# Three-layer graph convolution and neighbour dilation on one core: every engine held in program order, chained steps spread over the TensorE schedule, two comparisons made one

## The chip, the cores and the metric

The kernel runs on one core of one Trainium2 chip. The metric is device time in microseconds (us). A core has five engines that run side by side and meet at semaphores: TensorE (PE; its weight loads are listed as PEld), VectorE (DVE), ScalarE (ACT), GpSimd (POOL) and SyncE (SP), which here only issues DMAs. [...]

## The reference, cut to what matters

There are 16 graphs (batches) of 1024 nodes with 128 features, and for each a symmetric 1024 x 1024 adjacency matrix `adj`, about 6% filled.

```python
h = relu(layernorm(x))
for W, b, last in layer0:                 # 3 convolutions
    h = h @ W + b
    nh = h / max(|h|, 1e-12)
    h = (adj * (nh @ nh.T)) @ h           # relu unless last
x = x + h
h = relu(layernorm(x))
# dilation, row by row: of a row with num > 10 neighbours, those whose
# running count is a multiple of ceil(num / 2) are dropped, in row and column;
# later rows see it
adj_d = dilate(adj)
h1..h3 = three sage layers on adj_d       # batch norm after each
x = x + concat(h1, h2, h3) @ Wl + bl
```

## The kernel before, in words

**Two stages.** Stage one, up to line 720, holds all of layer 0 and all of the dilation, interleaved. Stage two, from line 723, holds the three sage layers; the change does not touch its code. The dilation depends on `adj` alone, so it fills engines while layer 0 keeps TensorE at work.

**Layer 0.** `order` lists 48 convolutions (16 batches in pairs, 3 layers each). A convolution goes through eight steps `s`, one for each block row `q` of the symmetric product, in the order `SEQ`. `products` (L290) multiplies on PE into PSUM `pg`, ACT copies `pg` to `g` (L311), and POOL multiplies `g` with the adjacency into `ew` (L312). `turn` (L320) transposes `g` on PE into PSUM `gt` (two buffers), and DVE multiplies it into the other part of `ew` (L330). `sums` and `sums_back` (L337, L353) multiply `ew` into the one PSUM tile `po`, three steps after the products (`LAG = 3`). After the last step ACT empties `po` (`hTo`, L368). Around this lie the transposes of the adjacency (`adjT_tile`, L216), which POOL stores to DRAM, the layer norm, the residual, and the features of the next convolution.

**The dilation.** It goes through 16 stretches: 8 row blocks `k`, each for two halves of 8 batches. A stretch has three parts. *Patterns*, 8 times: ACT makes the 0/1 pattern (L548, L549), PE transposes what earlier blocks kept (`pk`), DVE joins both (L554). *Rounds*, 2 to 6: DVE compares 8 tables (`E`, L611), PE counts (`pc`), DVE corrects `x` (L640). *Ranking*, 8 times: DVE subtracts the removals (L667), a DVE scan makes the running count `rank` (L670), ACT centres it (L671), DVE makes `kp` with two comparisons (L674, L677), POOL stores it as `keep` (L678).

**What sets the order.** `layer0()` and `dilation()` are generators. `layer0` yields the microseconds of PE work it just wrote (`COLS = 0.215` for a block of 128 columns, `TURN = 0.109` for a transpose), the dilation yields weights, and the loop at L701 writes layer-0 steps until they have caught up. So the program text is one interleaving. Only the PE calls of stage one are marked `keep_in_program_order` (L159 to L164). On DVE, ACT, POOL and SP a scheduler with its own idea of durations chose the final order.

Of the kernel before, what the change touches and what calls it, by code (L numbers as in the profile page):

```python
# [35 lines left out]
LAG = 3  # L36
# [6 lines left out]
T_DIL = 10  # L43


@with_exitstack
def tile_adj_preln_d2(
# [61 lines left out]
    def layernorm_relu(pool, dst, src, nm):  # L109

        st = pool.tile([P, NCH, 6], F32, tag="ln_st", name=f"ln_st_{nm}")
        mv = pool.tile([P, NCH, 2], F32, tag="ln_mv", name=f"ln_mv_{nm}")
        for c in range(NCH):
            nc.vector.bn_stats(st[:, c, :], src[:, c, :])
            nc.vector.bn_aggr(mv[:, c, :], st[:, c, :])
        rstd = pool.tile([P, NCH], F32, tag="ln_rstd", name=f"ln_rstd_{nm}")
        nc.scalar.activation(rstd, mv[:, :, 1], AF.Sqrt, bias=eps_col)
        nc.vector.reciprocal(rstd, rstd)
        nmr = pool.tile([P, NCH], F32, tag="ln_nmr", name=f"ln_nmr_{nm}")
        nc.vector.scalar_tensor_tensor(nmr, mv[:, :, 0], -1.0, rstd, ALU.mult, ALU.mult)  # L120
        for c in range(NCH):
            nc.scalar.activation(
                dst[:, c, :], src[:, c, :], AF.Relu, bias=nmr[:, c : c + 1], scale=rstd[:, c : c + 1]
            )

# [16 lines left out]
    def transposed(psum_pool, dst, src, nm, func=AF.Copy, halves=range(NHALF), transpose=nc.tensor.transpose):  # L142

        for h in halves:
            pt = psum_pool.tile([P, CPH, P], F32, tag="sm", name=f"pt_{nm}_{h}")
            for c in range(CPH):
                transpose(pt[:, c, :], src[:, h * CPH + c, :], ident)  # L147
            nc.scalar.activation(dst[:, h * CPH : (h + 1) * CPH, :], pt, func)


    with ExitStack() as actx:
# [6 lines left out]

        def matmul(*args, **kwargs):  # L159

            tc.keep_in_program_order(nc.tensor.matmul(*args, **kwargs))  # L161

        def transpose(*args):
            tc.keep_in_program_order(nc.tensor.transpose(*args))  # L164
# [12 lines left out]
        for fill, value, op in ((0.0, -2.0, ALU.is_ge), (4.0 * FAR, 2.0 * FAR, ALU.is_gt)):  # L177
            up = pool2.tile([P, NCH, P], F32, tag="tt", name=f"up_{fill}")[:, 0, :]
# [15 lines left out]
        mfl = pool2.tile([P, NCH, P], F32, tag="tt", name="mfl")[:NB, 0, :]  # L194
# [11 lines left out]

        adjA = pool1.tile([P, 2, NCH, N], F32, name="adjA")
        Nat = {}

        def adj_piece(b, q):  # L210
            Nat[b, q] = nat = pool2.tile([P, NCH, P], F32, tag="nat", name=f"nat_{b}_{q}")
            nc.sync.dma_start(
                nat, adj[b][:, q * P : (q + 1) * P].rearrange("(c p) q -> p c q", p=P)
            )

        def adjT_tile(b, q):  # L216

            t = adjA[:, b % 2, q, :]
            transposed(
                ps_sm, t.rearrange("p (c q) -> p c q", q=P), Nat.pop((b, q)), f"a{b}_{q}", transpose=transpose  # L220
            )
            nc.gpsimd.dma_start(adjT_d[b][q], t)

        class Batch:
# [6 lines left out]
            def fetch(self):  # L231
                b = self.b
                self.xb = pool2.tile([P, NCH, D], F32, tag="xb", name=f"xb_{b}_{self.l}")
                nc.sync.dma_start(self.xb, x[b].rearrange("(c p) d -> p c d", p=P))

            def norm(self):
                b = self.b
                self.h = pool2.tile([P, NCH, D], F32, tag="tt", name=f"h_{b}")
                layernorm_relu(pool2, self.h, self.xb, f"l0_{b}")

            def enter(self, h):
                if h == 0:
                    self.hT = pool2.tile([P, NCH, P], F32, tag="hT", name=f"hT_{self.b}")
                transposed(ps_sm, self.hT, self.h, f"h{self.b}", halves=(h,), transpose=transpose)

            def features(self, h):
# [6 lines left out]
                for c in range(CPH):  # L253
                    matmul(
                        pw[:, c, :], lhsT=self.hT[:, h * CPH + c, :], rhs=w0[:, l, :], start=True, stop=True
                    )
                if rn is None:
                    nc.vector.tensor_tensor(
                        self.hN[:, hc, :], pw, b0[:, l : l + 1, :].to_broadcast([P, CPH, P]), ALU.add
                    )  # L260
                else:
                    for c in range(CPH):
                        n = h * CPH + c
                        nc.vector.scalar_tensor_tensor(
# [3 lines left out]
            def turned(self):  # L268

                nhT = pool1.tile([P, NCH, P], F32, tag="nhT", bufs=2, name=f"nhT_{self.b}_{self.l}")  # L270
                transposed(ps_sm, nhT, self.hN, f"n{self.b}_{self.l}", transpose=transpose)
                self.next_nhT = nhT.rearrange("p c q -> p (c q)")

            def scaled(self):

                nm = f"{self.b}_{self.l}"
                hS = pool1.tile([P, NCH, D], F32, tag="hS", bufs=2, name=f"hS_{nm}")
                ss = pool2.tile([P, NCH], F32, tag="in_ss", name=f"ss_{nm}")
                for c in range(NCH):
                    nc.scalar.activation(hS[:, c, :], self.hN[:, c, :], AF.Square, accum_out=ss[:, c : c + 1])  # L280
                self.rn = inv_root(pool1, ss, nm)
                nc.gpsimd.tensor_tensor(
                    hS, self.hN, self.rn.unsqueeze(2).to_broadcast([P, NCH, D]), ALU.mult
                )
                self.next_hS = hS

            def begin(self):
                self.nhT, self.hS = self.next_nhT, self.next_hS

            def products(self, s):  # L290
# [9 lines left out]
                g = pool1.tile([P, most, P], F32, tag=f"g{s % 2}", name=f"g_{nm}")  # L300
                for c in range(0, row, CPH):
                    n = min(CPH, row - c)
                    pg = ps_g.tile([P, CPH, P], F32, tag="pg", name=f"pg_{nm}_{c}")
                    matmul(
# [6 lines left out]
                    nc.scalar.activation(g[:, c : c + n, :], pg[:, :n, :], AF.Copy)  # L311
                nc.gpsimd.tensor_tensor(  # L312
# [5 lines left out]
                return ew, g  # L318

            def turn(self, s, ew, g):  # L320
# [3 lines left out]
                for c in range(1, row, CPH):  # L324
                    n = min(CPH, row - c)
                    pt = ps_t.tile([P, CPH, P], F32, tag="gt", name=f"gt_{self.b}_{self.l}_{q}_{c}")
                    for i in range(n):
                        transpose(pt[:, i, :], g[:, c + i, :], ident)
                    at = row + c - 1
                    nc.vector.tensor_tensor(  # L330
# [6 lines left out]
            def sums(self, s, ew):  # L337

                q = SEQ[s]
                if s == 0:  # L340
                    self.po = ps_o.tile([P, N], F32, tag="po", name=f"po_{self.b}_{self.l}")
                for h in range(q // CPH, NHALF):
                    c = max(q, h * CPH)
                    n = (h + 1) * CPH - c
                    matmul(
# [7 lines left out]
            def sums_back(self, s, ew):  # L353
# [4 lines left out]
                for n in range(1, NCH - q):  # L358
                    matmul(
# [6 lines left out]
                if s == NCH - 1:  # L366
                    self.hT = pool2.tile([P, NCH, P], F32, tag="hT", name=f"hTo_{self.b}_{self.l}")
                    nc.scalar.activation(  # L368
# [4 lines left out]
            def residual(self):  # L373
                b = self.b
                self.x2 = x2 = pool2.tile([P, NCH, D], F32, tag="tt", name=f"x2_{b}")
                for h in range(NHALF):
                    pt = ps_sm.tile([P, CPH, P], F32, tag="sm", name=f"px_{b}_{h}")
                    for c in range(CPH):
                        transpose(pt[:, c, :], self.hT[:, h * CPH + c, :], ident)
                    for c in range(CPH):  # L380
                        n = h * CPH + c
                        nc.vector.scalar_tensor_tensor(
                            x2[:, n, :], pt[:, c, :], self.rn[:, n : n + 1], self.xb[:, n, :], ALU.mult, ALU.add
                        )
                nc.gpsimd.dma_start(x2_d[b].rearrange("(c p) d -> p c d", p=P), x2)

            def next_layer(self):
                b = self.b
                h0 = pool2.tile([P, NCH, D], F32, tag="tt", name=f"h0_{b}")
                layernorm_relu(pool2, h0, self.x2, f"l1_{b}")  # L390
# [649 lines left out]
```

## Time and profile before

| what | value |
|---|---|
| median of 3 runs | 3395.79 us (3391.37 to 3405.93) |
| profiled execution | 3385.13 us; its span on the core 3383.3 us |
| PE / DVE / ACT / POOL busy over the span | 2877.8 / 2105.8 / 1442.5 / 1052.7 us |
| stage one | 0 to about 2072 us of the span |
| PE / DVE / ACT / POOL busy, 0 to 2090 us | 1737 / 1417 / 1162 / 885 us |
| mean granted TensorE clock | 0.931 of full speed |

The span runs from the first to the last instruction; the run has 2 us around it. A group of instructions is listed by line, engine and operation, with its busy time and the mean time of one; the idle time behind it is that of the engine just before such an instruction. The granted clock is the share of full speed that TensorE was given.

### The profile page before, as it was taken

Reading aid. Unit: us, or ns where it says so; the run is one execution under the profiler, and the core shown is the slowest. Engines: PE = TensorE matmul, PEld = TensorE weight load, DVE = VectorE, ACT = ScalarE, POOL = GpSimd, SP = SyncE. Lnnn points to the kernel's source line nnn. Section 1 sums busy time; section 2 is a strip of 40 time slices with the busy share of each in tenths; the row PEclk is TensorE's granted clock in tenths of the full one; section 3 lists DMA queues with packets and bytes.
Section 4 is the critical chain, followed back from the end, with each engine's and each line's share of the span. In section 5 each row is a group of like instructions: output and inputs, shape, how many; then the busy total and the mean of one; then the engine's idle time right before and its main releaser. Section 6 shows DMA issues by size and latency. Waiting matters only on the chain. (4 is left out here: it accounts for less than half of the span.)

```text
span 3383.3 us, 53792 instructions
## 1 busy us (share of the span) xinstructions
PE 2877.8 (85%) x19811; PEld 2352.0 (70%) x19811; DVE 2105.8 (62%) x5319; ACT 1442.5 (43%) x3445; POOL 1052.7 (31%) x940
## 2 busy tenths in 40 slices
PE   6887888897797888788888897778887999989996
PEld 4655666565565665566656575777876899989996
DVE  2866767856867867876896733566666233345555
ACT  6746755655555545555645532011111322222223
POOL 2453444444344344444444443111211001000000
PEclk9998998998998999899899998889998999999998
DMA  8326336336336336427616303999997566656663
GB/s 279 120 84 219 122 112 223 102 113 208 102 105 208 121 101 214 135 90 222 198 43 193 129 1 117 352 345 354 351 353 278 181 205 203 204 181 225 225 224 125
DMA packets 436788, 623.10 MB, mean 184 GB/s; under 512 B 80080, under 2 KB 309328, under 8 KB 436512
## 3 DMA queue, kind: packets, MB, share of 16 engines
q1 hardware_dynamic: 349936, 416.87, 38.5%
q0 software_dynamic: 52288, 185.43, 14.3%
q10 hardware_dynamic: 34288, 17.24, 1.8%
q8 instruction: 158, 2.59, 0.3%
q14 instruction: 118, 0.97, 0.1%
HBM read 426.51 MB, written 192.94 MB: 183 GB/s over the span
## 5 line engine op out<-in xcount | busy, mean ns | idle before, releaser
L161 PE MATMUL po<-ew,hS 128*128 128x128 f32 (+3 forms) x3840 | 832.0, 353 | 68.5 <-ACT hTo L368 63.9
L312 POOL TENSOR_TENSOR ew<-g,adjA 128x1024 f32<-128x1024 f32 (+7 forms) x384 | 612.3, 1598 | 563.9 <-issue 262.5
L161 PEld LDWEIGHTS po<-ew,hS 128*128 128x128 f32 x3840 | 550.5, 199 | 212.1 <-issue 134.2
L161 PE MATMUL pg<-nhT 128*128 128x512 f32 (+3 forms) x1152 | 474.7, 523 | 23.9 <-ACT g L311 23.6
L963 PE MATMUL agg<-hw,aT 128*128 128x128 f32 x4096 | 472.0, 275 | 0.0
L963 PEld LDWEIGHTS agg<-hw,aT 128*128 128x128 f32 x4096 | 466.7, 192 | 4.0
L330 DVE TENSOR_TENSOR ew<-gt,adjA 128x512 f32<-128x512 f32 (+1 forms) x480 | 239.1, 522 | 252.8 <-PE gt L164 194.9
L311 ACT ACTIVATE g<-pg 128x512 f32<-128x512 f32 (+2 forms) x576 | 266.6, 484 | 209.1 <-PE pg L161 207.0
L670 DVE TENSOR_TENSOR_SCAN rank<-patt 128x1024 f16<-128x1024 f16 x128 | 315.7, 2475 | 0.1
L161 PEld LDWEIGHTS pg<-nhT 128*128 128x128 f32 x1152 | 203.3, 205 | 132.2 <-issue 95.7
L780 POOL TENSOR_TENSOR o<-o,rn_s 128x1024 f32<-128x1024 f32 x48 | 91.2, 1900 | 653.0 <-DVE rn_s L779 614.6
L164 PEld LDWEIGHTS gt<-ident,g 128*128 128x128 f32 x1344 | 170.0, 147 | 164.0 <-issue 90.4
L853 PE MATMUL agg<-hw,aT 128*128 128x129 f32 x2048 | 264.6, 288 | 15.9 <-DVE aT L830 15.9
L853 PEld LDWEIGHTS agg<-hw,aT 128*128 128x128 f32 x2048 | 254.7, 203 | 22.6 <-DVE aT L830 16.5
L164 PE MATMUL gt<-ident,g 128*128 128x128 f32 x1344 | 217.5, 284 | 50.9 <-DVE ew L330 49.7
L671 ACT ACTIVATE rank<-rank,fin 128x1024 f16<-128x1024 f16 x128 | 146.9, 1148 | 258.3 <-DVE rank L670 254.7
L830 DVE SCALAR_TENSOR_TENSOR aT<-raw,both 128x1024 f32<-128x1024 f32 x128 | 159.6, 1249 | 122.8 <-DMA raw<-adjT 121.3
L762 PE MATMUL pw<-wrx,hT 128*128 128x256 f32 x768 | 196.7, 409 | 10.8 <-ACT hT L916 9.7
L763 ACT ACTIVATE hw<-pw 128x256 f32<-128x256 f32 x192 | 73.8, 385 | 287.2 <-PE pw L762 268.1
L831 POOL DMA_DIRECT2D adT<-aT x128 | 69.3, 541 | 403.3 <-DVE aT L830 259.9
L164 PE MATMUL pt_a<-ident,nat 128*128 128x128 f32 x1024 | 155.4, 296 | 43.5 <-DMA nat<-in_adj_dram 11.8
L764 DVE TENSOR_TENSOR own<-pw,bs 128x256 f32<-128x256 f32 x192 | 78.7, 421 | 182.4 <-ACT hw L763 182.3
(166 smaller groups left out, 4412.7 us busy)
## 6 DMA issues: line engine op xcount, KB each, us to landing
aT<-adT SPq DMA_DIRECT2D x256, 512.0 KB, 4.3
nat<-in_adj_dram SPq DMA_DIRECT2D x128, 512.0 KB, 4.4
an<-in_adj_dram SPq DMA_DIRECT2D x128, 512.0 KB, 4.6
adjT<-adjA POOLq DMA_DIRECT2D x128, 512.0 KB, 4.7
raw<-adjT SPq DMA_DIRECT2D x128, 512.0 KB, 6.5
adT<-aT POOLq DMA_DIRECT2D x128, 512.0 KB, 7.1
keep<-kp POOLq DMA_DIRECT2D x128, 256.0 KB, 2.4
kb<-keep SPq DMA_DIRECT2D x128, 256.0 KB, 10.7
```

The source lines that it names most:

```text
L161: tc.keep_in_program_order(nc.tensor.matmul(*args, **kwargs))
L164: tc.keep_in_program_order(nc.tensor.transpose(*args))
L311: nc.scalar.activation(g[:, c : c + n, :], pg[:, :n, :], AF.Copy)
L312: nc.gpsimd.tensor_tensor(ew[:, :row, :], g[:, :row, :], self.aT[:, q, q * P :].rearrange("p (c q) -> p c q", q=P), ALU.mult,)
L330: nc.vector.tensor_tensor(ew[:, at : at + n, :], pt[:, :n, :], self.aT[:, q + c : q + c + n, q * P : (q + 1) * P], ALU.mult,)
L670: nc.vector.tensor_tensor_scan(rank, pt[:, 1 : N + 1], pt[:, 2:], 0.0, ALU.add, ALU.add)
L671: nc.scalar.activation(rank, rank, AF.Abs, bias=shift[:, i : i + 1])
L762: nc.tensor.matmul(pw[:, i, :], lhsT=hT[:, 2 * h + i, :], rhs=wrx[:, l, :], start=True, stop=True)
L780: nc.gpsimd.tensor_tensor(o, o, rn.unsqueeze(2).to_broadcast([P, NCH, D]), ALU.mult)
L830: nc.vector.scalar_tensor_tensor(aT, raw, 0.0, both, ALU.max, ALU.mult)
L853: nc.tensor.matmul(self.place(c), lhsT=aT[:, c * P : (c + 1) * P], rhs=self.hw[:, j, :], start=False, stop=j == NCH - 1 and (c % GA == GA ...
L963: nc.tensor.matmul(agg[:, c, :], lhsT=aT[:, c * P : (c + 1) * P], rhs=hw[:, j, :], start=False, stop=j == NCH - 1 and c % CPH == CPH - 1,)
```

## The change

- PE, DVE, ACT, POOL and SP of stage one are called through a wrapper that keeps each instruction in program order on its engine.
- Chains are cut in pieces. `later(us, do)` puts a piece on a heap, and it is written once the clock of yielded PE microseconds has passed that many microseconds. Layer norm, the squares and scale of a convolution, POOL's `ew` product, the tables, and the ranking (scan; centring 3.5 us later; comparison 6.0; store 8.5) are given out so. What is needed at once is forced out early (`upper()`, `part()`).
- `turn` comes two steps after `products` instead of one (`TURN_LAG = 2`), and the extras of a step now stand before `sums`.
- The two comparisons that made `kp` become one `scalar_tensor_tensor` that writes over `rank`. To allow it, three `[128, 8]` operations are added in each stretch and ACT's centring gets a scale. The 8 subtractions of a stretch become one operation for each unbroken run of pattern slots (1 or 2).
- The stores of `adjT`, `keep`, `x2` and `h0` move from POOL's queue to SP's.
- Buffers: `g` two for each parity instead of one, `an` and `kl` three instead of two (fetched two rows ahead), `rank` four; `T`, `Z`, `E`, `dT` and `x2` one instead of two. Layer norm writes in place, so the last batch's `x` is fetched again after the `If`.
- Weights: pattern 3.0 to 3.5 (its 2.5 and 1.0 for the tables go, and 4.0 after the eight come), round 5.0 + 1.0 to 5.0 + 0.5, ranking 3.5 + 2.0 to 6.0.

```diff
+class InOrder:
+    def __getattr__(self, name):
+        of = getattr(self._engine, name)
+        def call(*args, **kwargs):
+            got = of(*args, **kwargs)
+            if isinstance(got, bass.BassInstruction):
+                self._tc.keep_in_program_order(got)
+            return got
+        return call
...
+        PE, DVE = InOrder(tc, nc.tensor), InOrder(tc, nc.vector)
+        ACT, POOL, SP = InOrder(tc, nc.scalar), InOrder(tc, nc.gpsimd), InOrder(tc, nc.sync)
+        def later(us, do, *args):
+            left = [True]
+            def now():
+                if left:
+                    left.clear()
+                    do(*args)
+            if prompt:
+                now()
+            else:
+                heapq.heappush(waiting, (clock + us, count, now))
+            return now
...
-            nc.gpsimd.dma_start(adjT_d[b][q], t)
+                later(2.0, SP.dma_start, adjT_d[b][q], t)
...
-                nc.gpsimd.tensor_tensor(
+                upper = later(
+                    1.0,
+                    POOL.tensor_tensor,
...
                     if now:
                         behind.append((now, s, *now.products(s)))
-                        yield (NCH - q) * COLS
-                    late = None
-                    if len(behind) > LAG or not now:
-                        late, s_, ew, _ = behind.pop(0)
-                        late.sums(s_, ew)
-                        yield (NCH - SEQ[s_]) * COLS
-                    if s > 0 and now or s == 0 and i:
-                        b_, *of = behind[-2 if now else -1]
-                        if now or s == 0:
-                            b_.turn(*of)
-                            yield (NCH - 1 - SEQ[of[0]]) * TURN
-                    if late:
-                        late.sums_back(s_, ew)
-                        yield (NCH - 1 - SEQ[s_]) * COLS
+                        yield (NCH - SEQ[s]) * COLS
+                    at = -1 - TURN_LAG + (0 if now else s + 1)
+                    if at < 0 and -at <= len(behind):
+                        b_, *of = behind[at]
+                        b_.turn(*of)
+                        yield (NCH - 1 - SEQ[of[0]]) * TURN
+                    ...
+                    if len(behind) > LAG or not now:
+                        b_, s_, ew, _, upper = behind.pop(0)
+                        b_.sums(s_, ew, upper)
+                        yield (NCH - SEQ[s_]) * COLS
+                        b_.sums_back(s_, ew)
+                        yield (NCH - 1 - SEQ[s_]) * COLS
...
-            for i in range(BH):
-                nc.vector.tensor_tensor(pt[:, diag], pt[:, diag], E[:, i, :], ALU.subtract)
-                nc.vector.tensor_tensor_scan(rank, pt[:, 1 : N + 1], pt[:, 2:], 0.0, ALU.add, ALU.add)
-                nc.scalar.activation(rank, rank, AF.Abs, bias=shift[:, i : i + 1])
-                yield 3.5
-                nc.vector.tensor_scalar(
-                    kp, rank, low[:, i : i + 1], radius[:, i : i + 1], ALU.max, ALU.not_equal
-                )
-                nc.vector.tensor_tensor(kp, kp, pt[:, 2:], ALU.is_ge)
-                nc.gpsimd.dma_start(keep_d[b][cols, :], kp)
-                yield 2.0
+            while i < BH:
+                n = min(BH - i, SLOTS - slot(i))
+                here = patt[:, slot(i) : slot(i) + n, diag]
+                DVE.tensor_tensor(here, here, E[:, i : i + n, :], ALU.subtract)
+                i += n
+            def centered(i, rank):
+                ACT.activation(rank, rank, AF.Abs, bias=shift[:, i : i + 1], scale=unit[:, i : i + 1])
+            def keeps(i, rank):
+                DVE.scalar_tensor_tensor(
+                    rank, rank, radius[:, i : i + 1], pattern(i)[:, 2:], ALU.not_equal, ALU.is_ge
+                )
+            for i in range(BH):
+                DVE.tensor_tensor_scan(rank, pt[:, 1 : N + 1], pt[:, 2:], 0.0, ALU.add, ALU.add)
+                later(3.5, centered, i, rank)
+                later(6.0, keeps, i, rank)
+                later(8.5, SP.dma_start, keep_d[half * BH + i][cols, :], rank)
+                yield 6.0
```

## The prediction

> **What bounds the kernel now.** I first read the page's slices, to find stage one and what fills it.
>
> ```profile
> PE   6887888897797888788888897778887999989996
> ...
> DVE  2866767856867867876896733566666233345555
> ...
> PEclk9998998998998999899899998889998999999998
> ```
>
> A slice is 84.6 us; stage one is the first 24 and a half. PE is eight tenths busy there and never full. The chain of waits that ended last lies mostly in stage two (PE agg L963 13%), which the change leaves alone, so I read stage one by stretches. Scans (L670) mark ranking, table comparisons (L611) mark rounds. The sums by window (us, PE, PEld, DVE, ACT, POOL busy, clock, DMA share) show two rankings, two rounds, two patterns, and the tail of stage one, where the dilation is over.
>
> ```profile
> 409.00:451.00 42.00, 30.22 (x145) 20.25 (x144) 41.31 (x49) 17.50 (x38) 21.40 (x16) 0.88 0.11 42
> 907.00:944.00 37.00, 25.97 (x130) 17.68 (x128) 36.97 (x43) 15.77 (x28) 16.22 (x12) 0.91 0.11 43
> ...
> 860.00:907.00 47.00, 41.35 (x271) 29.36 (x269) 39.11 (x136) 29.14 (x94) 19.01 (x14) 0.96 0.24 73
> 1124.00:1169.00 45.00, 41.00 (x265) 28.98 (x266) 36.93 (x136) 28.48 (x89) 18.54 (x14) 0.96 0.26 80
> 1326.00:1366.00 40.00, 31.15 (x212) 23.09 (x210) 14.26 (x41) 26.40 (x78) 14.27 (x13) 0.94 0.89 283
> 1790.00:1824.00 34.00, 29.94 (x225) 22.66 (x224) 16.49 (x41) 18.54 (x60) 12.00 (x10) 1.00 0.77 227
> 1911.00:2072.00 161.00, 154.07 (x870) 111.46 (x868) 52.90 (x162) 66.28 (x202) 73.11 (x53) 1.00 0.07 23
> ```
>
> Ranking is DVE's: 98 to 100% busy, PE about 70% at a clock near 0.9. In rounds PE is near 90%, in patterns 78 to 88% with the DMA share up to 0.89. The tail runs at 96% and full clock: the layer-0 order alone can fill PE.
>
> I cut all of stage one so, and counted PE's matmuls in each part at full-clock price: 0.1116 us for 128 f32 columns (the chain has 8.93 us for 80 at clock 1.00), half for f16. Work over time: ranking 412 of 676 us (0.61), rounds with their ends 453 of 532 (0.85), patterns 537 of 656 (0.82), start 11 of 46, tail 156 of 161. Together 1569 us of work in 2072. The largest loss is ranking's 264 us.
>
> The groups by form give ranking's DVE cost; after the bar stand busy us and the mean ns of one.
>
> ```profile
> L670 DVE TENSOR_TENSOR_SCAN rank<-patt 128x1024 f16<-128x1024 f16 x128 | 315.7, 2475 | 0.1
> ...
> L677 DVE TENSOR_TENSOR kp<-kp,patt 128x1024 f16<-128x1024 f16 x128 | 120.5, 943 | 0.6
> ...
> L674 DVE TENSOR_SCALAR kp<-rank,th_f,fin 128x1024 f16<-128x1024 f16 x128 | 92.9, 727 | 5.6 <-ACT rank L671 2.7 <-DMA keep<-kp 2.3 <-ACT adjA L148 0.6
> ```
>
> The same lines with min/median/max show that the means hold waiting.
>
> ```profile
> L677 DVE TENSOR_TENSOR kp<-kp,patt x128: 634/678/2775, 109.3 to 1910.0; 128x1024 f16<-128x1024 f16 x128
> L674 DVE TENSOR_SCALAR kp<-rank,th_f,fin x128: 491/534/2847, 108.7 to 1908.2; 128x1024 f16<-128x1024 f16 x128
> L830 DVE SCALAR_TENSOR_TENSOR aT<-raw,both x128: 1210/1225/2078, 2108.3 to 2613.8; 128x1024 f32<-128x1024 f32 x128
> ```
>
> **Part 1: DVE in ranking.** Removed: 128 x (0.727 + 0.943) = 214 us. Added: 128 fused comparisons. No row has one on f16 with two SBUF inputs. The nearest is L830, the same instruction over as many elements: 1.225 median, and the scan's excess of mean over median, 0.20 (2.475 less its median 2.277), makes 1.42. The low bound is L677's median with that excess, 0.88; the high one L830's with L677's excess of 0.265, 1.49. At 1.42 it is 182 us, 32 saved (23 to 101). L667 took 128 x 0.391 = 50 us; some 30 joined subtractions, between L667's median 0.214 and L677's 0.678, make 13, so 37 saved. Three `[128, 8]` operations x 16 at 0.2 cost 10.
>
> [...]
>
> **Part 2: how much PE work lies in each stretch.** Dilation weights are spread over 0.96 x 48 x 28.0 = 1291 clock us; the new weights sum to 1685, so one is 0.766 us; PE's real price is 1.03 times the clock's. Ranking holds 128 x 6.0 x 0.766 x 1.03 = 606 us of work where the trace of before has 412. Rounds hold 62 x 5.5 plus 64 for their ends, 319, and with the counts on PE 344. Patterns hold 128 x 3.5 + 16 x 4.0 = 512, 404, and with `pk`, `pdt`, `pT` (960 f16 matmuls of 0.056) 458. With 156 and 11 this is 1575, beside 1569 counted.
>
> *Ranking.* DVE: scans 317, comparisons 182, subtractions 13, so 512 of its own. The convolutions' DVE rows inside the old rankings sum to 152 us for 412 of PE work, 0.369 each, so 224 for 606. Before, 568 + 152 = 720 us of rows took 676 (rows overlap a little), 0.939; 736 take 691. I add 2% for DVE finding nothing ready: 705 for 606 of work, a rate of 0.86.
>
> *Rounds.* One round's DVE rows: L497 0.387, L498 0.203, L605 0.365, L606 0.186, eight L611 at 151.1 / 496 = 0.305, L640 0.15: 3.73. With convolution work (0.369 x 4.2 = 1.55) and the counts with their hand-over (0.6) a round takes 5.9 us, 62 take 366; the ends 58 / 0.85 = 68. Together 434.
>
> *Patterns.* 458 at the old rate of 0.82: 559. ACT has 1.56 us a row for L548 and L549, and 0.62 per us of PE for the convolutions, 3.2 us against 3.2 of PE work, so the rate can't pass about 0.95 (482). The low bound is ranking's old 0.61 (751); I keep 0.82, since nothing on ACT or DVE is added here.
>
> *Start and end.* `x`, the mask and the first `nat` tile now share buffers, and the last batch's `x` is fetched after the `If` (4.2 us to landing). I take 8 us each, 0 to 15: 54 and 169.
>
> **Part 3: queues and waits.** Off POOL go 128 x 0.573, 128 x 0.578 and 31 of 0.94, 177 us of issuing, each of which waits for its source with later `ew` products behind it: POOL waited 179 us at L222 for ACT and 172 at L678 for DVE. PE waited for `ew` on POOL only 4.5 us and its weight loads 40, so I take nothing; bounds 0 to 40. SP takes these 288 issues at 0.34 to 0.44 us, 115 us in 1900 on a queue that is not the bound. Behind a store that waits for `keeps` stand the next `an`, `kl` and `nat` loads.
>
> The waits (us in all, times, longest) name the other places; the first is ACT's, which now keeps its place ahead of later `g` copies.
>
> ```profile
> ACT rank L671 <- DVE rank L670: 254.7, 107, 7.1
> ...
> PE po L161 <- ACT hTo L368: 63.9, 30, 6.7
> ...
> PE gt L164 <- DVE ew L330: 49.7, 27, 8.2
> ```
>
> For `po` the built order shows only the 0.43 us product of step 3 between the last `sums_back` and the next first `sums`, as before, but in half of the convolutions an adjacency, residual or entry transpose now stands there too: a quarter of 63.9, 15, gained (0 to 45). The new `turn` place costs slack: for `q = 1`, between `turn` and `sums_back` lay 5.8 clock us, now 2.5. Whatever DVE holds then, a scan or the E comparisons, delays PE. In rounds and ranking this is inside the DVE sums; in patterns DVE is 40% busy with pieces up to 1.1 us. No row shows this order; from -60 (the scheduler's order cost more) to +254 (the rival below), I take +20.
>
> **The sum.** Before 676 + 532 + 656 + 46 + 161 = 2071. After 705 + 434 + 559 - 15 + 54 + 169 + 20 = 1926. Gain 145: 3385 - 145 = 3240 for the profiled execution, which lay 10.7 under the median of its runs, so 3250 for the runs.
>
> **The rivals.** *DVE's program order stalls PE (slower).* At each `turn` with transposes, 48 x 7 = 336, the product for `ew` stands behind what DVE was given before, and 2.5 us are left. With a 3.73 us burst ahead, 1.4 for the product and its hand-over, and the `turn` anywhere in 3.83 clock us, PE waits max(0, 2.68 - u), 0.94 on average. At every `turn` this is 316 us, of which 62 (one a round) are counted: 3250 + 254 = 3504. It decides from 145 / 336 = 0.43 us a `turn`. For it: DVE's saturation in ranking, and 8.2 us as the longest wait of `gt`. Against: bursts are cut in halves, and DVE is half idle outside ranking and rounds.
>
> *SP's one queue makes the loads late.* Patterns move up to 0.89 of the DMA's time; two rows ahead is 6.5 us against 4.6 to landing. One us for each of 128 rows: 3378.
>
> *The fusion does nothing* (1.67 for 1.42): 3282.
>
> *PE fills up.* Patterns at 0.95 (482), rounds at 0.9 (382), no loss for order: 3250 - 77 - 52 - 20 = 3101.
>
> **How the numbers follow.** A measurement of this kernel can tell about 0.5%, 17 us. Forecast 0.50, fusion without effect 0.08, PE full 0.12, SP's queue 0.08 (some of it within 17 us), order stalls 0.22. Likeliest time 3250. The range takes the unknown costs downwards (101 instead of 32 for the fusion, 45 for `po`) to about 3120; upwards it reaches past SP's queue into the milder order stalls, 3420, and leaves out the rest of the full-PE and stall cases, under 2 in 10. Faster 0.73, within 0.06, slower 0.21.
>
> **What would show it.** Right: scans end near 1760 us instead of 1899; rankings still with DVE above 95% but PE at 80% or more; the fused comparison between 1.2 and 1.5 us; POOL without DMA issues. Wrong: PE waiting for DVE at `po` or `gt` for more than 150 us in all, ACT's `patt` waiting for `an` well over its 103 us of before, or patterns with a lower PE share than before.

## The result, and the profile after

The changed kernel takes 3406.06 us (median; 3399.79 to 3415.59) beside 3395.72 of the kernel before in the same series: ratio 1.0036, interval [1.0022, 1.005]. That is no gain but a loss of some 0.4% (0.2 to 0.5), where a gain of 145 us had been forecast. The profiled execution has a span of 3404.2 us.

The slices of its page (engine, then 40 slices in tenths) hardly differ from those of before; stage one still ends in slice 25:

```profile
PE   5887787897888888898888897778887899989996
...
DVE  1866678677777787876786833666666333345555
...
PEclk8999999999998999899898998888888899999998
```

The windows (from:to and length in us; busy us of PE, PEld, DVE, ACT, POOL; clock; DMA share and GB/s) show two rankings, a stretch of six rounds, patterns, a stretch of three rounds, and the tail.

```profile
919.60:968.90 49.30, 43.67 (x236) 30.86 (x236) 48.30 (x64) 30.40 (x79) 24.56 (x13) 0.97 0.12 42
1044.90:1102.60 57.70, 46.59 (x253) 34.01 (x252) 49.72 (x87) 35.36 (x79) 23.04 (x10) 0.87 0.68 218
1002.20:1044.90 42.70, 34.44 (x210) 25.74 (x211) 30.94 (x107) 11.64 (x28) 9.55 (x7) 0.84 0.29 87
...
1102.60:1143.00 40.40, 33.98 (x231) 25.37 (x230) 20.72 (x64) 28.14 (x73) 10.26 (x7) 0.97 0.90 277
1261.00:1278.40 17.40, 15.27 (x96) 10.97 (x95) 16.88 (x56) 6.06 (x11) 6.74 (x4) 0.93 0.19 60
1943.10:2086.00 142.90, 138.70 (x781) 100.83 (x782) 48.86 (x141) 55.43 (x169) 65.27 (x45) 1.00 0.06 18
```

A ranking now carries about 250 matmuls of PE instead of 130 to 145, so the work did move as the new text says. But a ranking grew from 42 us in the mean (676 / 16) to 53 (850 / 16), and in the second one VectorE is busy for 49.72 of 57.70 us and PE for 46.59: neither is full. In the third line, the stretch of six rounds, PE idles for 8 of 43 us and the granted clock is 0.84. All of stage one cut this way (work is PE's matmuls at full-clock price, as in the prediction):

| stretch | before: us / work | forecast | after: us / work |
|---|---|---|---|
| start | 46 / 11 | 54 | 50 / 11 |
| patterns | 656 / 537 | 544 / 458 | 582 / 465 |
| rounds | 532 / 453 | 434 / 344 | 462 / 307 |
| ranking | 676 / 412 | 705 / 606 | 850 / 644 |
| tail | 161 / 156 | 169 / 156 | 143 / 141 |
| order | | 20 | |
| sum | 2071 | 1926 | 2087 |

The work landed within 38 us of where the weights were to put it; the price of ranking was wrong by 145 us. Its own rows on VectorE, by form (busy us, mean ns), and the same by tile (min/median/max ns). L57 is the line of the wrapper, through which all of stage one is called now, so rows are told apart by their tiles:

```profile
L57 DVE TENSOR_TENSOR_SCAN rank<-patt 128x1024 f16<-128x1024 f16 x128 | 323.4, 2528 | 0.2
...
L57 DVE SCALAR_TENSOR_TENSOR rank<-rank,fin,patt 128x1024 f16<-128x1024 f16 x128 | 210.9, 1648 | 6.2 <-ACT rank L57 6.1
```

```profile
L57 DVE TENSOR_TENSOR_SCAN rank<-patt x128: 2232/2280/4092, 113.7 to 1935.0; 128x1024 f16<-128x1024 f16 x128
...
L57 DVE SCALAR_TENSOR_TENSOR rank<-rank,fin,patt x128: 1225/1283/3461, 121.0 to 1941.9; 128x1024 f16<-128x1024 f16 x128
```

The fused comparison takes 1.28 us undisturbed and 1.65 in the mean; 128 of them sum to 211 us, the two that it replaced to 214. The timeline of the longest (start, us) shows what stretches it, first VectorE, then POOL:

```profile
962.87 3.46 DVE L57 SCALAR_TENSOR_TENSOR rank<-rank,fin,patt 128x1024 f16<-128x1024 f16 x1
```

```profile
962.89 2.35 POOL L57 TENSOR_TENSOR ew<-g,adjA 128x1024 f32<-128x1024 f32 x1 [2.42 <-ACT g L57]
```

POOL's product ends at 965.24; the comparison ends 1.09 us later, most of its own 1.28. It is listed as running from 962.87, but ends as if it had done next to nothing until POOL was through. Of the 128, 52 last over 12% above the median; each of the 52 began while a POOL product ran or, as this one, within 0.03 us of its start, and ends 1.08 us after it (median). The scan does the same (37 of 37, end 2.15 us after POOL's). The features' sums `hN`, whose first operand lies in PSUM, begin while a product runs 130 times and are never longer (excess over the median -0.2 us in all). In sum VectorE's rows in stage one did not shrink: 1651 us before, 1652 after, where the prediction had taken 59 us off them.

PE's own waits (us in all, times, longest) stayed small, as the prediction had wanted, and ACT's wait for the row loads, which the rival on SP's queue would have raised above its 103.2 us, fell:

```profile
PE po L57 <- DVE ew L57: 36.2, 15, 4.2
PE gt L57 <- DVE ew L57: 35.8, 27, 4.4
PE pt_a L57 <- ACT adjA L57: 31.8, 15, 11.9
PE po L57 <- ACT hTo L57: 27.8, 24, 4.0
PE pc L57 <- DVE E L57: 21.0, 18, 2.4
```

```profile
ACT patt L57 <- DMA an<-in_adj_dram: 9.1, 6, 3.3
```

### The profile page after: what moved, and what is told of

Its sections match the earlier page's. It is cut to its first block, busy times and chain, and to the rows that moved or that the text cites. A ratio compares the mean times of both kernels' runs of the same rounds, so it can differ in the third digit from the quotient of the medians.

```text
span 3404.2 us, 53301 instructions
## 1 busy us (share of the span) xinstructions
PE 2892.6 (85%) x19811; PEld 2358.8 (69%) x19811; DVE 2153.4 (63%) x5136; ACT 1450.5 (43%) x3444; POOL 925.7 (27%) x652
## 5 line engine op out<-in xcount | busy, mean ns | idle before, releaser
L57 POOL TENSOR_TENSOR ew<-g,adjA 128x1024 f32<-128x1024 f32 (+7 forms) x384 | 650.2, 1696 | 1225.3 <-ACT g L57 541.0
L57 PE MATMUL po<-ew,hS 128*128 128x128 f32 (+3 forms) x3840 | 811.6, 359 | 64.2 <-DVE ew L57 36.2
L57 PEld LDWEIGHTS po<-ew,hS 128*128 128x128 f32 x3840 | 566.6, 203 | 248.0 <-issue 149.0
L57 PE MATMUL pg<-nhT 128*128 128x512 f32 (+3 forms) x1152 | 464.3, 513 | 14.1 <-ACT g L57 13.9
L57 ACT ACTIVATE g<-pg 128x512 f32<-128x512 f32 (+2 forms) x576 | 265.0, 485 | 448.3 <-PE pg L57 418.1
L57 DVE TENSOR_TENSOR ew<-gt,adjA 128x512 f32<-128x512 f32 (+1 forms) x480 | 237.4, 519 | 205.0 <-PE gt L57 175.7
L57 DVE TENSOR_TENSOR_SCAN rank<-patt 128x1024 f16<-128x1024 f16 x128 | 323.4, 2528 | 0.2
L57 PEld LDWEIGHTS pg<-nhT 128*128 128x128 f32 x1152 | 198.4, 200 | 116.7 <-issue 91.7
L57 PEld LDWEIGHTS gt<-ident,g 128*128 128x128 f32 x1344 | 163.8, 144 | 112.0 <-DVE ew L57 53.0
L57 PE MATMUL gt<-ident,g 128*128 128x128 f32 x1344 | 210.7, 279 | 35.9 <-DVE ew L57 35.8
L57 DVE SCALAR_TENSOR_TENSOR rank<-rank,fin,patt 128x1024 f16<-128x1024 f16 x128 | 210.9, 1648 | 6.2 <-ACT rank L57 6.1
L57 PE MATMUL pt_a<-ident,nat 128*128 128x128 f32 x1024 | 155.8, 294 | 67.0 <-ACT adjA L57 31.8
L57 PEld LDWEIGHTS pt_a<-ident,nat 128*128 128x128 f32 x1024 | 126.3, 151 | 84.1 <-ACT adjA L57 35.6
```

What stands on the lines that cost most here:

```text
L57: got = of(*args, **kwargs)
```

## The experiments

Three theories. **Order**: holding VectorE, ACT, POOL and SP in program order costs what the rest of the change brings. **Exclusion**: VectorE rows with two SBUF inputs and POOL's products keep each other out, as the 52 comparisons and 37 scans above suggest, and the forecast did not price that. **Place**: the work was put where it is dear. The kernel before measured 3398 to 3402 us in the series below; all differences "against after" are from 3406, though the runs come from several series, between which the kernel before moved by up to 7 us.

### The fusion

`b_fused` is the kernel before with the fused comparison:

```diff
-                nc.vector.tensor_scalar(
-                    kp, rank, low[:, i : i + 1], radius[:, i : i + 1], ALU.max, ALU.not_equal
-                )
-                nc.vector.tensor_tensor(kp, kp, pt[:, 2:], ALU.is_ge)
+                nc.vector.scalar_tensor_tensor(
+                    kp, rank, radius[:, i : i + 1], pt[:, 2:], ALU.not_equal, ALU.is_ge
+                )
```

> The kernel before, with the fused comparison alone (its three [128, 8] operations and ACT's scale with it). Theory A (VectorE operations with two SBUF inputs and POOL's products exclude each other, so a fused comparison pays 1.28 us by itself plus a wait for POOL, 1.65 in all as in the changed kernel): 128 x (1.65 - 1.67) is nothing, the three operations add at most 10 us of VectorE time, so 3396 to 3406 us, ratio 1.000 to 1.003. The prediction's step (1.42 us): 32 - 10 us of VectorE saved, 3374, ratio 0.993.

Measured 3392.84 us, 0.9984 [0.9965, 1.0004]. `a_unfused` does the reverse to the changed kernel:

```diff
-                DVE.scalar_tensor_tensor(
-                    rank, rank, radius[:, i : i + 1], pattern(i)[:, 2:], ALU.not_equal, ALU.is_ge
-                )
+                DVE.tensor_scalar(
+                    rank, rank, low[:, i : i + 1], radius[:, i : i + 1], ALU.max, ALU.not_equal
+                )
+                DVE.tensor_tensor(rank, rank, pattern(i)[:, 2:], ALU.is_ge)
```

> The changed kernel with the two comparisons in place of the fused one, and without the three [128, 8] operations and ACT's scale. Theory A: two short operations that each wait for POOL against one long one; 0.73 + 0.94 against 1.65, so equal within 10 us, 3396 to 3412. The prediction's step: 32 us more VectorE time less 10 for the three operations, and ranking bound by VectorE, 3428. Theory B (program order and the chain's due times are what costs): a second hand-over-free operation adds nothing, 3406.

Measured 3408.02 us, 1.0028 [1.0013, 1.0044], where after has 1.0036. So no gain of the fusion can be measured in either order; the interval of `b_fused` allows at most 12 us, and the prediction's step was worth 22. In `b_fused` the comparison took 1.419 us, just the forecast's 1.42, and saved 32 us of rows; but the scans beside it rose from 2.475 to 2.621 us, 19 us in all, and VectorE's rows in stage one sum to 1670 us instead of 1651.

### The order

`a_free` gives four engines back to the scheduler and keeps the new text, with PE's program the same to the instruction:

```diff
-        PE, DVE = InOrder(tc, nc.tensor), InOrder(tc, nc.vector)
-        ACT, POOL, SP = InOrder(tc, nc.scalar), InOrder(tc, nc.gpsimd), InOrder(tc, nc.sync)
+        PE, DVE = InOrder(tc, nc.tensor), nc.vector
+        ACT, POOL, SP = nc.scalar, nc.gpsimd, nc.sync
```

> The changed kernel with only PE held in program order; DVE, ACT, POOL and SP are given back to the scheduler, everything else as in the changed kernel. Theory B (program order on these four engines eats the 145 us that were forecast): the time falls, to 3330 or less. Theory A (the exclusion of POOL and VectorE bounds ranking whatever the order): within 30 us of the changed kernel, 3376 to 3436, with the scheduler drawing the scans together again, so that less layer-0 work lies in the rankings (nearer 412 than 644 us) and each block of a ranking is nearer 5.3 us than 6.6.

Measured 3343.51 us, 0.9835 [0.9816, 0.9854]: 62 us under after, 54 under the kernel before. Twice a stretch of rounds and the ranking behind it:

```profile
814.80:859.80 45.00, 38.28 (x250) 27.26 (x249) 37.47 (x162) 27.11 (x88) 14.18 (x10) 0.97 0.36 107
859.80:896.00 36.20, 27.40 (x124) 18.34 (x123) 36.04 (x26) 16.67 (x26) 17.31 (x7) 0.85 0.14 51
940.40:982.60 42.20, 36.48 (x262) 26.99 (x260) 33.74 (x112) 16.63 (x46) 13.03 (x9) 1.00 0.25 86
982.60:1020.20 37.60, 25.47 (x118) 17.27 (x118) 37.47 (x47) 21.50 (x32) 10.88 (x5) 0.83 0.61 196
```

The scheduler drew the scans together again: rankings hold 392 us of work in 624, rounds 417 in 504, patterns 586 in 673 (0.87, against 0.80 in after and 0.82 before). Neither theory's time was met, order's being 3330 or less. Which engine? `a_dvefree` frees only `DVE` (the first line of that diff), `a_dveheld` only the second line.

> The changed kernel with VectorE alone given back to the scheduler; PE, ACT, POOL and SP stay in program order. Theory D (of the 62 us that program order costs, VectorE's order has nearly all: layer-0 products that PE waits for stand behind scans, and count corrections behind products): 3345 to 3360 us. Theory Q (the queues of ACT, POOL and SP have it: copies for PE behind centring and patterns): within 15 us of 3406.

> The counterpart: ACT, POOL and SP are given back to the scheduler, PE and VectorE stay in program order. Theory D: 3390 to 3410 us. Theory Q: 3345 to 3360. If each has a part, both come out between; if the orders only work together, both stay near 3406 and only freeing all four gains.

Measured 3378.70 us, 0.9943 [0.9923, 0.9962], and 3390.97, 0.9973 [0.9959, 0.9988]: 27 and 15 us, together less than the 62 of both at once. Neither expectation for `a_dvefree` was met. VectorE has the larger share, and freeing the others is worth more when VectorE is free too.

`a_prompt` keeps program order and takes the due times away, which moves the matmuls of the tables in PE's order too:

```diff
-        clock, waiting, count, prompt = 0.0, [], 0, False
+        clock, waiting, count, prompt = 0.0, [], 0, True
```

> The changed kernel with every step of a chain written at once (no due times), all five engines still in program order. Theory O (in program order a waiting step holds its whole engine, and the due times are what keeps that small): the comparison stands right behind the scan and waits for ACT's 1.24 us and two hand-overs, some 1.5 us x 128, and POOL's product and the norms stand behind their sources too: 3550 us or more. If the due times carry nothing: 3390 to 3425.

Measured 3785.54 us, 1.1132 [1.1117, 1.1146]. VectorE's longest entry among its waits, and PE's:

```profile
DVE rank L57 <- ACT rank L57: 174.8, 114, 3.6
```

```profile
PE pg L57 <- ACT g L57: 133.9, 40, 6.9
```

In after they are 6.1 and 13.9 us. Given out in microseconds, the chains save 380 us of what program order would cost.

`a_lag1` puts `turn` back to one step after `products`:

```diff
-TURN_LAG, LAG = 2, 3
+TURN_LAG, LAG = 1, 3
```

> The changed kernel with `turn` one step after `products`, as before the change (TURN_LAG 1), which gives VectorE's product 5.8 instead of 2.5 clock us before `sums_back` asks for it. If the short slack of that place is what program order costs (TensorE's idle time before po is 46 us and before gt 23 us in the rankings): 3350 to 3385 us. If TensorE then waits at gt for ACT's copies of g instead: 3406 to 3440.

Measured 3388.36 us, 0.9966 [0.9953, 0.9978], 18 under after. The wait for `ew` goes from `po` to `gt`, whose entry grows to this, and PE's idle time before `po` in the rankings falls from 46 to 8 us:

```profile
PE gt L57 <- DVE ew L57: 97.2, 32, 5.5
```

Before `gt` it grows there from 22 to 68 us, by more than that. The time lies between both expectations, and where the 18 us come from is not shown.

### The exclusion

`a_memset` lets POOL write a constant in place of the product:

```diff
                 upper = later(
                     1.0,
-                    POOL.tensor_tensor,
-                    ew[:, :row, :],
-                    g[:, :row, :],
-                    self.aT[:, q, q * P :].rearrange("p (c q) -> p c q", q=P),
-                    ALU.mult,
+                    POOL.memset, ew[:, :row, :], 0.02
                 )
```

> The changed kernel with POOL's product for the upper part of ew replaced by a memset of the same tiles to 0.02 (the product is left out, so that POOL reads no SBUF there; POOL also no longer waits for ACT's g). Theory A: scans fall from a mean of 2.53 to 2.3 us, the fused comparison from 1.65 to 1.3, the comparisons E from 0.31 to 0.27, VectorE's sum in stage one by 100 us or more; the rankings from 850 us to some 705 (what VectorE's own rows make of them), and the run to 3200 to 3270. Theory B: the waits of the order stay, the run loses 40 us at most, 3360 or more, though the rows get shorter.

Measured 3252.98 us, 0.9562 [0.954, 0.9584]: 153 less than after. VectorE's rows (`E` had a mean of 373 ns in after), and the same stretches as in the first three window lines of after:

```profile
L57 DVE TENSOR_TENSOR_SCAN rank<-patt 128x1024 f16<-128x1024 f16 x128 | 297.0, 2322 | 0.2
...
L57 DVE SCALAR_TENSOR_TENSOR rank<-rank,fin,patt 128x1024 f16<-128x1024 f16 x128 | 164.9, 1288 | 6.2 <-ACT rank L57 6.0
```

```profile
L57 DVE TENSOR_SCALAR E<-T,th,at 128x128 f16<-128x128 f16 x496 | 118.4, 333 | 1.7
```

```profile
865.90:909.90 44.00, 39.99 (x222) 28.16 (x222) 41.40 (x64) 29.36 (x78) 9.59 (x13) 1.00 0.15 52
973.90:1026.60 52.70, 43.05 (x266) 32.17 (x265) 45.44 (x87) 36.17 (x85) 8.85 (x10) 1.00 0.76 240
941.10:973.90 32.80, 29.29 (x206) 22.40 (x206) 25.38 (x107) 10.61 (x22) 5.11 (x8) 0.95 0.36 113
```

The waits in scans and comparisons are nearly gone (means 2.32 and 1.29, after's medians within 0.05). Rankings take 777 us for the same 643 of work, 72 more than expected; rounds 396 for 310, patterns 568. `E` keeps part of its waits: 37 of its rows are still lengthened, by 12 us in all, and each of them met a memset. Nor need all of the gain be exclusion: a memset has no wait for ACT's `g`, POOL's stage-one time falls from 754 to 322 us, and PE multiplies constants. Against the constants as the reason for the higher clock speaks that in the patterns, where PE is busy for 87% of the time instead of 86%, the clock is 0.97 in both. `b_memset` is the same on the kernel before, `a_free_memset` on `a_free`.

> The kernel before with the same memset of 0.02 in place of POOL's product (the product is left out). Theory A1 (the exclusion costs the kernel before as much as the changed one): 150 us less, 3235 to 3260 us. Theory A2 (the changed kernel pays more for it, since 644 instead of 412 us of layer-0 work, with its products, lie in the rankings): 60 to 110 us less, 3285 to 3340, so that without the exclusion the change would have been a gain of 30 us or more.

> The changed kernel with only PE in program order and POOL's product replaced by a memset of 0.02 (the product is left out). If exclusion and order are two separate costs, they add: 3406 - 62 - 153 = 3191 us, 3175 to 3210. If the order only hurts because the exclusion makes rows late: 3225 to 3253.

Measured 3273.88 us, 0.964 [0.9613, 0.9667], which lies between the two expectations: 125 less; and 3230.08, 0.9496 [0.9482, 0.951], where two separate costs would have given 3191. Without the products, then, the change is a gain of 21 us, and freeing the engines is worth 23 instead of 62: 39 us of what program order costs go away with the products. That this is by way of rows that run late was the expectation's reading; it is not shown apart from POOL's shorter work.

`a_split` keeps the product and cuts it in pieces, which leaves POOL more to do:

```diff
+                    for c in range(0, row, 2):
+                        n = min(2, row - c)
+                        POOL.tensor_tensor(ew[:, c : c + n, :], g[:, c : c + n, :], aq[:, c : c + n, :], ALU.mult)
```

> The changed kernel with POOL's product for the upper part of ew in pieces of at most two blocks (0.72 us by its row) instead of one of up to 2.35 us; the same elements, some 0.18 us more for each of about 580 added instructions, 104 us on POOL, which is not the bound. Theory W (what costs is the length of one wait: VectorE waits for the whole product that it meets, and everything in program order behind it): waits over the median of the scan, the fused comparison and E fall from 111 us to half or less, and the run to 3340 to 3380 us. Theory S (the sum counts, both engines want the time): 3400 to 3440, the added POOL time being paid in waits.

Measured 3355.34 us, 0.9879 [0.9857, 0.99]: 51 less, with 975 us of products on POOL instead of 756. By form:

```profile
L57 POOL TENSOR_TENSOR ew<-g,adjA 128x256 f32<-128x256 f32 x768 | 718.9, 961 | 982.0 <-ACT g L57 603.6 <-issue 336.7 <-DVE E L57 11.6
...
L57 DVE TENSOR_TENSOR_SCAN rank<-patt 128x1024 f16<-128x1024 f16 x128 | 311.1, 2431 | 0.2
...
L57 DVE SCALAR_TENSOR_TENSOR rank<-rank,fin,patt 128x1024 f16<-128x1024 f16 x128 | 186.6, 1458 | 12.3 <-ACT rank L57 12.0
```

The pieces take 0.96 us against 0.73 in the median, so POOL now pays in waits and VectorE less: scans, comparisons and `E` hold 70 us over after's medians instead of 111, VectorE's stage-one sum falls from 1652 to 1577 us. The expectation had the waits fall to half or less; 63% stayed, while the time fell as expected. So what POOL needs in sum is not what costs here; how far the gain comes from shorter single waits and how far from the smaller sum of VectorE's waits is not told apart. That an earlier first piece also helps PE can't be excluded by this run. `b_split` does the same to the kernel before.

> The kernel before with POOL's product in pieces of at most two blocks. Theory W for any order: 30 to 55 us less, 3345 to 3370. Length mattering only where VectorE is held in program order or drawn close by the new text: 3385 to 3415.

Measured 3376.93 us, 0.9935 [0.9913, 0.9956], 25 less and between both expectations: half as much as in the changed kernel.

### The place of the work

`a_even` changes weights alone:

```diff
-                yield 3.5
+                yield 3.7
...
-                    yield 5.0
+                    yield 7.5
...
-                yield 6.0
+                yield 4.2
```

> The changed kernel with other weights alone: ranking 4.2 for 6.0, round 7.5 + 0.5 for 5.0 + 0.5, pattern 3.7 for 3.5, which puts some 440 us of layer-0 work in the rankings and 440 in the rounds, near the kernel before. If what was lost is the place of the work (rounds too empty, rankings too full): 3335 us, ratio 0.98. If it is program order itself: rankings near 700 to 740 us, the run within 15 us of 3406.

Measured 3419.02 us, 1.0057 [1.0035, 1.0079]. Work lies nearer to the kernel before (ranking 485, rounds 457, patterns 477; before 412, 453, 537), and the stretches take 735, 584 and 585 us. The rounds are the plain case: 457 of work in 584 us where the kernel before had 453 in 532. Putting the work back did not bring the time back, so its place was not the loss.

`a_free_spread` and `b_spread` set SPREAD from 0.96 to 1.04, on `a_free` and on the kernel before.

> The changed kernel with only PE in program order and SPREAD 1.04 for 0.96, so that the tail's 163 us of layer-0 work at a rate of 0.97 shrink to some 40 and go to rankings, rounds and patterns. If a us of work costs 0.5 to 0.75 us there (from the kernel before to the changed one, rankings took 232 us more work for 174 us): 30 to 60 us below 3343, 3285 to 3315. If the stretches are full: 3335 to 3360.

> The kernel before with SPREAD 1.04 alone. If less tail helps by itself as it did on the changed kernel with free engines (12 us): 3375 to 3392. If the kernel before has no room in its stretches: 3395 to 3410.

Measured 3331.19 us, 0.979 [0.9773, 0.9806], and 3393.65, 0.9983 [0.9968, 0.9999]: 12 and some 6 us. The tail of 49 us shows that the work moved; it cost nearly as much elsewhere.

### Versions that beat both kernels

All three are `a_free` with SPREAD 1.04; `a_free_lag1` has TURN_LAG 1, `a_free_split` pieces of two blocks, `a_free_split1` pieces of one.

> Only PE in program order, SPREAD 1.04 and TURN_LAG 1, to be compared with 3331 us. PE's program keeps its order in both, so if the slack behind turn is a matter of PE's place for it: 18 us less as in program order, 3305 to 3322. If the slack only mattered because VectorE was held: 3325 to 3340.

> Only PE in program order, SPREAD 1.04 and the product in pieces of two blocks, to be compared with 3331 us. Theory W with the wait's length mattering only in program order: 3325 to 3345. Length mattering on its own: 3280 to 3315. Theory S: 3340 to 3370.

> Only PE in program order, SPREAD 1.04, the product in pieces of one block (0.45 us each, 1728 of them, 786 us of POOL against some 690 in pieces of two). If the length of a wait still counts: 3275 to 3290 us. If the added POOL time and the added meetings eat it: 3298 to 3340.

Measured 3337.16 us, 0.9818 [0.98, 0.984]; 3297.54, 0.9711 [0.9689, 0.9734]; and 3279.47, 0.9641 [0.9615, 0.9666]. The first shows that the 18 us of TURN_LAG were there only while the four engines were held. The second is what length on its own was to give. The last is the fastest kernel that leaves nothing out, 3.6% under the kernel before: the new text, PE alone in order, and short POOL products.

## Why the prediction was wrong

**The fused comparison (1.42 us, 32 saved).** Measured 1.648 in the changed kernel, outside the bounds of 0.88 to 1.49. The excess over the median was taken from the kernel before (0.20); with more products of POOL in the rankings it was 0.37, and in the old order 1.419 came true (`b_fused`). Undisturbed it takes 1.28 us where the two that it replaced take 0.53 + 0.68 by their medians in the kernel before, and neither `b_fused` nor `a_unfused` shows a gain of the fusion. The rival "the fusion does nothing" was right in its part, at its 1.67. The 10 us of the three added operations were worked out but never entered the prediction's sum; they turned out small (rows `fin` 22.1 us before, 23.3 after).

**Ranking, 705 us (the step that failed).** 850 were measured. 38 us more work than reckoned explain 13 of it (606 to 644, at 0.369 x 0.939 x 1.02). Then the rows: 842 us in the rankings where the prediction's prices give 512 + 238 = 750 for 644 of work. The comparison is 29 of these 92, the scan 7, and the convolutions' rows 57, since they cost 0.458 us for one of work instead of 0.369. That figure was taken from the old rankings, where the scheduler had moved part of such rows into the patterns (0.43 there); over stage one of before it is 0.40. The products are not behind this term: without them (`a_memset`) it is still 0.44. What lifts it from 0.40 to 0.46 stays open. At the step's own 0.939 and 2%, 842 of rows make 806. The last 44 are VectorE finding nothing ready far more often than the 2% allowed: it was busy in 91% of the time, where the forecast's sign asked for above 95%, and PE in 83%. In the old rankings it was 96% over all sixteen, not the 98 to 100% of the two windows in the prediction. Two engines that are loaded nearly alike and hand work to each other in a fixed order were each taken to reach their own limit; here neither did. Even without the products PE had 87% and VectorE 88%.

**Rounds, 434 us.** 462 for less work than forecast. PE waits 34 us before the counts `pc` (21 of them for `E`, 12 for ACT's `adjA`) and 13 before `gt`; without the products the stretches take 396 us and the wait before `pc` is 7. The 3.73 us of a round's rows had been summed from means that held the waits of before, and only 0.6 us a round was taken for the counts and their hand-over.

**Patterns, 544 us for 458.** 582 for 465: the rate is 0.80, not 0.82. The wait at `po` for `hTo` did fall, from 63.9 to 27.8 us, more than the 15 that were taken off, but no shorter patterns came of it. Start and tail came out 4 and 26 us better.

**Order, +20.** It had the widest bounds, -60 to +254, and no row to choose by; `a_free` measures 62 us in the changed kernel. The first rival, program order on VectorE, had the mechanism but not the size: 254 were worked out, freeing VectorE alone gives 27, all four 62. (Its 62 that were counted already are a number of rounds; at 0.94 us each they are 58.) Its waits of PE at `po` and `gt` for VectorE are 72 us, under the 150 that the prediction had named as its sign, so that sign was set too high for a loss of 62. Of the signs for the forecast, POOL without DMA issues and PE above 80% in the rankings came true; the scans end at 1937 us instead of near 1760, VectorE is under 95%, and the patterns' rate fell, one of the signs against. The rival on SP's queue did not happen: ACT waited 9.1 us for `an` instead of 103.2. Nor did PE fill up: it was busy for 85% of the span, as before.

**The exclusion itself.** The runs show it for scans and comparisons: the scan's mean is 2.53 us beside products and 2.32 beside memsets, the fused comparison's 1.65 and 1.29. What the sum lacked was that scans and comparisons paid for it alike, and `E` too, with one f16 tensor (all 26 of its lengthened rows in after met a product, and the 37 of `a_memset` met memsets), and POOL's products in their turn (129 us over the shortest of each size in after, 81 before). That two inputs in SBUF are what decides was the theory's part and is not shown: `hN`, with one in PSUM, was never lengthened, but `E` was. One thing eased: in the kernel before, 17 of the 47 lengthened `E` rows had begun while POOL issued a DMA, and those issues are gone. Taking the products out gives 153 us on the changed kernel and 125 on the one before, so the change pays 28 more for them, which turns the gain of 21 us that it is without the products into a loss of about the size that was measured. The 153 us are also the size of the missing gain, but that is a coincidence of sizes: the kernel before would gain most of it too. How far the 153 are exclusion proper, and how far POOL's shorter chain, stays open; `a_split`, with the products kept, gained 51.

## What to carry to other kernels

Before two engines are packed more densely, look whether their rows lengthen each other: compare mean with median by tile, and see in the timeline what ran on the other engine; then shorten the instruction that is waited for, which here gave 51 us where fusing the waiting one gave none. PE was held in program order in every run, so what that is worth is not shown here; for the other four engines a scheduler's order beat a planned text by 62 us, and a text without due times lost 380. A stretch in which two coupled engines were both to be nearly full did not come out at the busier one's sum: in after's rankings the busier one reached 91%, with the other at 83%. In `a_free`, where the scheduler lets VectorE reach 99% of the rankings, PE has 73%.

## What was not expected of the hardware

Less idle time on PE went with a higher clock, so it gained more than itself. From the changed kernel to `a_memset` the span shrinks by 148.6 us, and 64.7 of these are PE's own busy time for the same 19811 matmuls (2892.6 to 2827.9): the mean granted clock rose from 0.931 to 0.951. The same stretch of rounds went from clock 0.84 to 0.95, the second ranking from 0.87 to 1.00. The runs that keep the products show it too: in the profiled executions `a_split` has 62 us less span and 23.5 less PE time than after (clock 0.940), `a_free` 69 and 42 (0.941), and `a_prompt`, with PE busy for 79% of its span, has a clock of 0.895. The idle share alone did not set the clock: at 83% busy, after's rankings had 0.93 and its rounds 0.88.

With POOL's products cut in pieces, POOL took longer in sum and the kernel less time: 756 to 975 us of products and 3406.06 to 3355.34 in all with pieces of two blocks (`a_split`), 1165 us of products with pieces of one (`a_free_split1`, 3279.47 where `a_free_spread` takes 3331.19). By after's medians, 0.46 us for one block and 0.73 for two, some 0.18 us of a piece is fixed; this is an estimate from two sizes.
